# A two-layer metaformer on one core: the second convolution's weights are made between layer 0's expert tiles, and expert results load by half strips

## The chip, the cores and the metric

The kernel runs on one core of a Trainium2 chip. The metric is device time of one execution in microseconds (us). The time before is the median of three runs, 1847.21 us (1844.24 to 1854.55).

## The reference, cut to what matters

The input is x, (2, 256, 56, 56) in float32. Two layers follow each other; both add to x.

```python
# layer 0
x = x + attention(ln_c(x))                # 7x7 window attention, 8 heads
t = to_tokens(x)                          # (2, 3136, 256)
t = t + moe0(ln_t(t))                     # 8 experts, top 2: out = tokens + sum_e weight_e * expert_e(tokens)
x = from_tokens(t)
# layer 1
x = x + conv_block(ln_c(x))               # below
t = to_tokens(x)
t = t + moe1(ln_t(t))                     # 8 experts of width 512, top 2
x = from_tokens(t)

def noised_tri_conv(x, w):                # w: (256, 256, 3, 3)
    tq = ternary_quantize(w - mean(w))    # -1, 0 or 1, thresholds from the extremes of all of w
    return conv3x3(x, tq) + einsum('bchw,oc->bohw', x, tq[:, :, 1, 1])   # centre tap counts twice

def conv_block(x):
    out1 = relu(batch_norm(noised_tri_conv(x, w1)))
    out2 = batch_norm(noised_tri_conv(out1, w2))
    return relu(out1 + out2)
```

## The kernel before

The picture is cut into 14 strips of 8 rows (448 positions, four blocks of 112 tokens). The kernel goes through these stages: attention by strips; layer 0's experts; the first convolution; the second convolution; layer 1's routing by strips; layer 1's experts; the output.

**Layer 0's experts.** Tokens are sorted to their experts through memory, and 56 tiles of 256 rows are worked off one after another (`experts_in_order`). For each tile TensorE transposes (pt, L1073), ScalarE copies to ut (L1077), TensorE makes ph (L1105), ScalarE applies gelu into h (L1112), TensorE makes py (L1122), VectorE adds the bias into y (L1130), and GpSimd scatters y's rows to ys (L1132). The order of SyncE, VectorE, TensorE and ScalarE is that of the program here (`manual_schedule`). py has two buffers and y five.

**The ternary weights between the tiles.** From the tile on at which routing is done, `beside` advances the generator `prepare` by four steps after each tile. It runs `ternary` for w1, then for w2: each loads the weights piece by piece into space that later holds strips, takes their extremes and sum (L1250, L1252, L1255), and turns them into -1, 0 and 1 (L1286 to L1290). The end of `ternary` depends on the target. For w1 (four components of F(2,3)) it makes the transformed weights in bf16 (L1302 to L1309). For w2 the target has three components, and two ScalarE copies per 128x2304 (L1297) move the plain taps to `sums[1]` in bf16.

**The first convolution** (`conv`, L1771) works on pairs of strips in the row-wise form F(2,3): 28 steps, four components for each of seven pairs. `component` makes v on GpSimd (L1765), hi on ScalarE (L1766, the part of v that the fast matmul format holds) and lo = v - hi on VectorE (L1767); 24 matmuls (L1792) follow, and VectorE or ScalarE adds their result up in x (L1811 to L1820). v, hi and lo have two buffers each. Its own weights are cast to wq by ScalarE before (L1776).

**Combining beside it.** The strips come into being beside the steps. `combine(i)` reads the middle state x_mid, loads the expert results of a strip, 896 KB, in one DMA (`gathered`, L1172; three buffers `got`), adds them with their weights (`add_up`: on VectorE, L1191; for strip 2 on ScalarE, L1183, and GpSimd, L1186), takes the statistics of each token, normalizes into xn (L726; two buffers), transposes on TensorE (L1200) and copies into the padded picture pad (L1748). Strips 0 to 2 come before the first step, strips 3 and 4 during the first two steps, and then two strips for each pair of strips that is convolved. SyncE's order is that of the program; that of the other engines is chosen at compile time, in general the earliest in the program among what is ready.

**The second convolution** (`conv43`, L1844) uses F(4,3) with six components, on groups of 2, 4, 4 and 4 strips: 24 steps. Its weights wq4 (36,864 bytes a partition) are made by `weights43` (L1823), called at step 26 of the first convolution, once the pool of `combine` is closed: a GpSimd add (L1831), two ScalarE multiplies (L1833, L1834) and five VectorE passes (L1835 to L1839) over 128x1536. Between the convolutions `affine` makes scale and shift from the statistics (L1970 to L1977), and `between` (L2028) writes the rectified strips to pad on ScalarE. In a step, VectorE (with GpSimd for some parts) makes p, q, r, s and from them v in PSUM (two buffers), ScalarE hi (L1902) and VectorE lo (L1903); both have three buffers and are prepared two steps ahead. Their pool, conv_c2, takes the place of the first convolution's.

**After it**, `residual` reads x_mid again into back (L2068) and adds the transposed result to it (L2087).

Pools of fast memory are placed at both ends of the space and opened and closed like stacks, so that a tile that lies on an earlier one waits for that one's last use. On the low side, from the bottom: x_all, pad, sums[1] (134,592 to 143,808), the small tiles of the raw pool (to 145,376), conv_w1 with wq (to 169,952), conv_c1 with two each of hi, lo and v, 3,712 bytes each (to 192,224). On the high side, from 229,344 down: conv_t with got and xn (to 196,096), and after it wq4 (to 192,480). During layer 0's tiles the high side reaches down to 174,496, where the buffers xg begin.

Of the kernel before, what the change touches and what calls it, by code (L numbers as in the profile page):

```python
# [10 lines left out]
F32 = mybir.dt.float32  # L11
F32R = mybir.dt.float32r
# [620 lines left out]
def metaformer(ctx: ExitStack, tc: tile.TileContext, a: dict, out: bass.AP, flag):  # L633
# [532 lines left out]

        add_up(i, gathered(i, ys, tp, bufs), wgt, xt)

    def gathered(i, ys, tp, bufs=2):
        rows = NTT * TOP * TT  # L1170
        y = tp.tile([TT, NTT, TOP, C], F32, tag="got", name="got", bufs=bufs)
        nc.sync.dma_start(  # L1172
            y, ys[i * rows : (i + 1) * rows, :].rearrange("(p t j) c -> p t j c", t=NTT, j=TOP)
        )
        return y

    def add_up(i, y, wgt, xt, away=False):

        if away:
            for j in range(TOP):  # L1180
                for t in range(NTT):
                    n = i * NTT + t
                    nc.scalar.activation(  # L1183
                        y[:, t, j, :], y[:, t, j, :], AF.Copy, scale=wgt[:, j, n : n + 1]
                    )
                nc.gpsimd.tensor_tensor(xt, xt, y[:, :, j, :], ALU.add)  # L1186
            return
        for t in range(NTT):
            n = i * NTT + t
            for j in range(TOP):  # L1190
                nc.vector.scalar_tensor_tensor(  # L1191
                    xt[:, t, :], y[:, t, j, :], wgt[:, j, n : n + 1], xt[:, t, :], ALU.mult, ALU.add
                )

    def channels(ps, tag, xt):
# [34 lines left out]
    def ternary(name, sums, ps_pool, tag, tp, at):  # L1230

        size = KC * TAPS * C
        wide = NTT * C
        raw = x_all.rearrange("p s c -> p (s c)")[:, at * wide : at * wide + size]
        parts = [(n, raw[:, n : n + PART]) for n in range(0, size, PART)]

        def load(i):
            n = min(wide, size - i * wide)
            nc.sync.dma_start(raw[:, i * wide : i * wide + n], a[name + "_flat"][:, i * wide : i * wide + n])

        st3 = tp.tile([P, 3, len(parts)], F32, tag="st3", name="st3")
        load(0)
        for i, (n, part) in enumerate(parts):
            if n % wide == 0 and n + wide < size:
                load(n // wide + 1)
            nc.vector.tensor_reduce(st3[:, 0, i : i + 1], part, AX.X, ALU.max)  # L1250
            yield
            nc.vector.tensor_reduce(st3[:, 1, i : i + 1], part, AX.X, ALU.min, negate=True)  # L1252
            yield
            low = tp.tile([P, PART], F32, tag="low", name="low", bufs=1)
            nc.scalar.activation(low, part, AF.Copy, accum_out=st3[:, 2, i : i + 1])  # L1255
        st = tp.tile([P, 3], F32, tag="st", name="st")
        nc.vector.tensor_reduce(st[:, 0:2], st3[:, 0:2, :], AX.X, ALU.max)
# [12 lines left out]
        nc.vector.scalar_tensor_tensor(  # L1270
            lo, ext[:, 1:2], -1.0, mean, ALU.mult, ALU.subtract
        )
        span = tp.tile([P, 1], F32, tag="w_span", name="w_span")
        rest = tp.tile([P, 1], F32, tag="w_rest", name="w_rest")
        nc.vector.tensor_tensor(span, hi, lo, ALU.subtract)
        nc.vector.tensor_scalar_mul(third, span, 1.0 / 3.0)


        nc.vector.scalar_tensor_tensor(rest, third, -2.0, span, ALU.mult, ALU.add)
        nc.vector.tensor_tensor(rest, rest, third, ALU.subtract)  # L1280
        nc.vector.scalar_tensor_tensor(third, rest, 1.0 / 3.0, third, ALU.mult, ALU.add)
        nc.vector.tensor_tensor(lo, lo, third, ALU.add)
        nc.vector.tensor_tensor(hi, hi, third, ALU.subtract)
        for n, part in parts:
            low = tp.tile([P, PART], F32, tag="low", name="low", bufs=1)
            nc.vector.tensor_scalar(low, part, mean, lo, ALU.subtract, ALU.is_lt)  # L1286
            yield
            nc.vector.tensor_scalar(part, part, mean, hi, ALU.subtract, ALU.is_gt)
            yield
            nc.vector.tensor_tensor(part, part, low, ALU.subtract)  # L1290
            yield
        g = raw.rearrange("p (k y c) -> p k y c", k=KC, y=3)
        middle = g[:, :, 1, C : 2 * C]
        nc.vector.tensor_scalar_mul(middle, middle, 2.0)
        if sums.shape[2] == 3:
            for k in range(KC):
                nc.scalar.copy(sums[:, k], g[:, k])  # L1297
                yield
            return
        for k in range(KC):  # L1300
            up, middle, down = (g[:, k, y, :] for y in range(3))
            nc.scalar.copy(sums[:, k, 0, :], up)  # L1302
            nc.scalar.copy(sums[:, k, 3, :], down)
            nc.vector.tensor_tensor(up, up, down, ALU.add)
            yield
            nc.vector.tensor_scalar_mul(middle, middle, 0.5)
            yield
            for c, op in ((1, ALU.add), (2, ALU.subtract)):
                nc.vector.scalar_tensor_tensor(sums[:, k, c, :], up, 0.5, middle, ALU.mult, op)  # L1309
                yield  # L1310
# [4 lines left out]
    with ExitStack() as st:  # L1315
# [330 lines left out]
        def routed_all():  # L1646
# [32 lines left out]

            some = x_all[:, len(STRIPS) - 3 :].rearrange("p s c -> p (s c)").bitcast(BF16)  # L1680
            sums.append(some.rearrange("p (k n c) -> p k n c", k=KC, n=COMPS))
            sums.append(wqp.tile([P, KC, 3, 3 * C], BF16, tag="sums", name="sums"))

        def prepare():
            for i in range(2):
# [24 lines left out]
    with mid:  # L1710

        with ExitStack() as st:
# [20 lines left out]
            def combine(i):  # L1733

                xt = XT[STRIPS[i]][:TT]
                if i >= X_FIRST:
                    nc.sync.dma_start(xt, x_mid[i])
                got = gathered(i, ys[0], tp, 3)
                yield
                add_up(i, got, wgt0, xt, i == X_FIRST - 1)  # L1740
                yield
                rstd, nmr = yield from token_stats(tp, xt, eps6, True)
                xn = tp.tile([TT, NTT, C], F32, tag="xn", name="xn")
                scaled(xn, xt, rstd, nmr)
                yield
                pu = channels(strips_ps, "pu", xn)
# [73 lines left out]
                                nc.vector.bn_stats(stats[:, o, i, :], X[STRIPS[i]][:, o, :])  # L1820
                return stats

            def weights43(taps):  # L1823

                wp2 = st.enter_context(
                    tc.tile_pool(name="conv_w2", bufs=1, side="right", reuse_waits="tile")
                )
                w = wp2.tile([P, KC, COMPS4, 3 * C], F32R, tag="wq4", name="wq4")
                g = [taps[:, :, y, :] for y in range(3)]

                nc.gpsimd.tensor_tensor(w[:, :, 4, :], g[0], g[2], ALU.add)  # L1831
                both = w[:, :, 4, :].bitcast(F32)
                nc.scalar.mul(w[:, :, 0, :], g[0], 1.5)  # L1833
                nc.scalar.mul(w[:, :, 5, :], g[2], 6.0)  # L1834
                nc.vector.tensor_tensor(w[:, :, 1, :], both, g[1], ALU.add)  # L1835
                nc.vector.tensor_tensor(w[:, :, 2, :], both, g[1], ALU.subtract)
                nc.vector.scalar_tensor_tensor(g[0], g[0], 0.25, g[2], ALU.mult, ALU.add)
                for c, by in ((3, 0.5), (4, -0.5)):
                    nc.vector.scalar_tensor_tensor(  # L1839
                        w[:, :, c, :], g[1], by, g[0], ALU.mult, ALU.add  # L1840
                    )
                return w

            def conv43(wq, cp, vps, tp, at_step):  # L1844
# [6 lines left out]
                def component(u, c):  # L1851
# [20 lines left out]
                    def banks(ap):  # L1872
                        return ap[:, :n].rearrange("p (a r) k w -> p a (r k w)", r=4)

                    hi, lo = tile_of("hi", F32R, 3), tile_of("lo", F32R, 3)
                    pv = vps.tile([P, 2, 512], F32, tag="v", name="pv")
                    v = pv[:, : n // 4, : 4 * KC * WC]
                    if c == 1:
# [108 lines left out]
            def combining(n):  # L1987
# [18 lines left out]
                if late < 2 and 5 <= i < len(STRIPS):  # L2006
                    coming.append(combine(i))
                push_all()
                if n == COMPS * UNITS - 2:
                    assert not coming  # L2010
                    strips_on.close()
                    wq4.append(weights43(sums[1]))

            wq4 = []

            with tc.manual_schedule(engines={mybir.EngineType.SP}):
                stats = conv(sums[0], combining)
            scale, shift = affine(stats, bn["g1"], bn["b1"], rp)
            first_on.close()
            cp = st.enter_context(tc.tile_pool(name="conv_c2", bufs=2, reuse_waits="tile"))  # L2020
            vps = st.enter_context(tc.tile_pool(name="conv_vs", bufs=2, space=PSUM, reuse_waits="tile"))

# [17 lines left out]
                    for i in FOURS[u + 1]:  # L2040
                        between(i + 1)

            stats = conv43(wq4[0], cp, vps, rp, rectifying)
            scale2, shift2 = affine(stats, bn["g2"], bn["b2"], rt, eps5_36)
        wq_held.close()

# [244 lines left out]
```

## Time and profile before

| | |
|---|---|
| median of three runs | 1847.21 us |
| profiled execution | 1852.05 us, its span 1850.1 us |
| mean granted TensorE clock | 0.874 of full speed |
| TensorE busy (matmuls) | 1530.3 us, 83% of the span |
| VectorE busy | 979.4 us, 53% |
| ScalarE busy | 696.1 us, 38% |
| GpSimd busy | 655.1 us, 35% |
| DMA | 291.77 MB, mean 158 GB/s |

The stages, read from the timeline: attention to about 515 us, layer 0's tiles to 841, first convolution to 1040, second convolution to 1182, layer 1's routing to 1390, layer 1's experts to 1770, output to 1850.

A row of a timeline gives the start in us, the duration, the engine (PE is TensorE, DVE VectorE, ACT ScalarE, POOL GpSimd, SP SyncE), the line, the operation, its output and inputs by name and shape, and in brackets the idle time before it and what ended that. In the chain of waits each row is a piece of the one path that ended last. In a table of stretches the columns are the stretch, its length, then the busy time and the instruction count of PE, PEld, DVE, ACT and POOL, then the granted clock, the share of the DMA engines and GB/s.

### The profile page before, as it was taken

What the parts mean: (1) busy time and instruction counts of PE and PEld (TensorE: products, weight loads), DVE (VectorE), ACT (ScalarE), POOL (GpSimd) and SP (SyncE); (2) the same over time, 40 slices, a digit from 0 to 9 for tenths busy, and PEclk for the clock granted to TensorE, in tenths of its full rate; (3) what the DMA queues carried; (4) which work ended last, traced back from release to release, by engine and by line L of the source; (5) the groups of instructions that cost most, each with busy time, mean ns of one, the idle gap of its engine ahead of it and who ended that gap; (6) DMA issues with size and microseconds to landing.
All of it is one profiled execution on the core that took longest, in us unless ns stands there. A gap on an engine that the chain in (4) does not pass through costs nothing.

```text
span 1850.1 us, 25838 instructions
## 1 busy us (share of the span) xinstructions
PE 1530.3 (83%) x8612; PEld 1199.4 (65%) x8612; DVE 979.4 (53%) x2688; ACT 696.1 (38%) x1358; POOL 655.1 (35%) x664
## 2 busy tenths in 40 slices
PE   6999998999778669894899799666348999999963
PEld 3555555555467557783788688555337888888842
DVE  4467566465645337845999788666432111111136
ACT  3454442434333324643444532344213333333312
POOL 3112534335333654442344143164562222222210
PEclk9999988999889879995999899755558999999975
DMA  7022333213267667885551000133544778788758
GB/s 244 22 83 82 113 90 112 62 52 93 60 205 229 230 208 263 307 256 156 158 163 53 1 1 1 40 112 98 170 136 152 270 265 270 262 279 277 274 161 301
DMA packets 91886, 291.77 MB, mean 158 GB/s; under 512 B 20487, under 2 KB 35803, under 8 KB 80416
## 3 DMA queue, kind: packets, MB, share of 16 engines
q1 hardware_dynamic: 66736, 231.79, 40.5%
q0 software_dynamic: 21200, 51.82, 8.0%
q10 hardware_dynamic: 3808, 6.42, 1.0%
q8 instruction: 70, 1.15, 0.3%
q14 instruction: 72, 0.59, 0.1%
HBM read 218.51 MB, written 74.20 MB: 158 GB/s over the span
## 4 chain that ended last, share of the span: by engine, by line
PE 52%; DVE 21%; DMA 8%; issue 7%; another core or an unknown queue 5%; POOL 4%; ACT 3%; SPq 0%; POOLq 0%; ACTq 0%; DVEq 0%
PE ph L1105 14%; PE py L1122 12%; PE av L1486 5%; PE sc L1457 3%; PE pj L1409 3%; DVE x L1191 3%; PE pw L1556 3%; PE pv L1431 3%; PE pl L784 2%; PE pt L1073 2%; DMA got<-ys 2%; DMA out<-o_out 2%; DVE oc L1543 2%; DVE t_stats L705 2%
## 5 line engine op out<-in xcount | busy, mean ns | idle before, releaser
L1105 PE MATMUL ph<-ut,w 128*128 128x256 f32 (+1 forms) x1472 | 320.3, 370 | 28.2 <-issue 20.3
L1130 DVE TENSOR_TENSOR y<-py,w 128x512 f32<-128x512 f32 (+1 forms) x120 | 76.8, 640 | 439.2 <-PE py L1122 379.2
L1122 PE MATMUL py<-w,h 128*128 128x256 f32 x1288 | 298.8, 380 | 0.0
L1105 PEld LDWEIGHTS ph<-ut,w 128*128 128x128 f32 x1472 | 258.2, 200 | 59.8 <-issue 22.4
L870 POOL DMA_INDIRECT xs<-u,pos x224 | 217.1, 969 | 168.0 <-issue 87.0
L1122 PEld LDWEIGHTS py<-w,h 128*128 128x128 f32 x1288 | 244.8, 192 | 33.1
L1132 POOL DMA_INDIRECT ys<-y,dest x136 | 136.3, 1003 | 274.8 <-DVE dest L1080 185.5
L1112 ACT ACTIVATE h<-ph,w 128x256 f32<-128x256 f32 (+1 forms) x368 | 162.3, 447 | 131.2 <-PE ph L1105 82.2
L1476 ACT ACTIVATE ex<-sc 112x476 f32<-112x476 f32 (+3 forms) x224 | 116.7, 570 | 207.8 <-PE sc L1466 174.9
L1077 ACT COPY ut<-pt 128x512 f32<-128x512 f32 (+1 forms) x120 | 65.2, 543 | 302.5 <-PE pt L1073 244.9
L1486 PE MATMUL av<-ex,vals 112*64 112x238 f32 (+3 forms) x896 | 124.1, 397 | 17.8 <-DVE acc L1496 14.3
L1792 PE MATMUL pc<-lo,wq 128*128 128x448 f32 x336 | 132.2, 395 | 6.5 <-DVE lo L1767 6.4
L1496 DVE TENSOR_TENSOR acc<-av,acc 128x238 f32<-128x238 f32 (+3 forms) x224 | 87.8, 407 | 87.5 <-PE av L1486 65.3
L1792 PE MATMUL pc<-hi,wq 128*128 128x448 f32 x336 | 131.7, 394 | 2.0 <-DVE x L1816 1.8
L1132 POOL DMA_INDIRECT ys<-y,to x81 | 82.3, 1016 | 135.0 <-DVE dest L1080 76.4
L1191 DVE SCALAR_TENSOR_TENSOR x<-got,wgt,x 112x256 f32<-112x256 f32 x216 | 102.3, 544 | 30.4 <-DMA got<-ys 30.4
L1935 PE MATMUL pc<-hi,wq 128*128 128x448 f32 (+1 forms) x288 | 104.4, 371 | 15.9 <-ACT hi L1902 9.4
L1935 PE MATMUL pc<-lo,wq 128*128 128x448 f32 (+1 forms) x288 | 103.6, 368 | 0.2 <-DVE lo L1903 0.2
L1457 PE MATMUL sc<-q_im,keys 32*112 32x238 f32 (+3 forms) x896 | 94.3, 427 | 9.5 <-ACT ex L1476 5.7
L1486 PEld LDWEIGHTS av<-ex,vals 112*64 112x64 f32 x896 | 55.9, 141 | 67.7 <-issue 25.2
L1765 POOL TENSOR_TENSOR v<-pad 128x928 f32<-128x928 f32 (+1 forms) x28 | 56.4, 2028 | 99.4 <-DVE lo L1767 49.1
L1073 PE MATMUL pt<-ident,xg 128*128 128x128 f32 x434 | 71.7, 287 | 15.5 <-ACT ut L1077 10.4
(273 smaller groups left out, 2479.7 us busy)
## 6 DMA issues: line engine op xcount, KB each, us to landing
w<-in_L_experts SPq DMA_DIRECT2D x64, 1154.0 KB
w<-in_L_experts SPq DMA_DIRECT2D x56, 641.0 KB
xg<-xs SPq DMA_DIRECT2D x97, 260.0 KB
got<-ys SPq DMA_DIRECT2D x28, 896.0 KB
acc<-in_fresh SPq DMA_DIRECT2D x14, 896.0 KB
xt<-in_x_tok SPq DMA_DIRECT2D x14, 448.0 KB
xr<-in_x_tok SPq DMA_DIRECT2D x14, 448.0 KB
rec<-shares SPq DMA_DIRECT2D x28, 224.0 KB
```

Source lines behind the costliest of these rows:

```text
L870: w = nc.gpsimd.indirect_dma_start(xs[:, :], bass.IndirectOffsetOnAxis(ap=pos[:, j, t0 + t : t0 + t + 1], axis=0), us[t // NTT][:, t % NTT ...
L1073: nc.tensor.transpose(pt[:, k, i * P : (i + 1) * P], d["xg"][:, i, k * P : (k + 1) * P], ident)
L1105: nc.tensor.matmul(ph[:, :g], w1[:, k, f * P : (f + 1) * P], d["ut"][:, k, :g], start=k == 0, stop=k == KC - 1,)
L1112: nc.scalar.activation(d["h"][:, f, :g], ph[:, :g], AF.Gelu, bias=b1[:, f : f + 1])
L1122: nc.tensor.matmul(py[:, i, :], d["h"][:, f, i * P : (i + 1) * P], w2[:, f, :], start=f == 0, stop=f == NF - 1,)
L1132: o = nc.gpsimd.indirect_dma_start(ys[:, :], bass.IndirectOffsetOnAxis(ap=d["to"][:, i : i + 1], axis=0), y[:, i, :], None, bounds_check=T ...
L1191: nc.vector.scalar_tensor_tensor(xt[:, t, :], y[:, t, j, :], wgt[:, j, n : n + 1], xt[:, t, :], ALU.mult, ALU.add)
L1457: nc.tensor.matmul(sc[h // 2][:, h % 2, :nq], keys[g][p, c, tx * TT : (tx + 1) * TT], q_im[p, c, r0:r1, c0:c1], start=True, stop=False,)
L1476: nc.scalar.activation(e[:, :, :nq], sc[j][:, :, :nq], AF.Exp, scale=HD**-0.5)
L1486: nc.tensor.matmul(av[VW * i : VW * (i + 1), :nq], vals[g % 3][:, tx, 2 * c + j, 2 * i : 2 * i + 2, :].rearrange("p a d -> p (a d)"), ex[j ...
L1792: nc.tensor.matmul(pc[:, :NT], wq[:, k, c, dx * C + o * P : dx * C + (o + 1) * P], part[:, :, k, dx : dx + W], start=m == 0, stop=m == 2 * ...
L1935: nc.tensor.matmul(pc[:, : 2 * ns * W], wq[:, k, c, dx * C + o * P : dx * C + (o + 1) * P], part[:, : 2 * ns, k, dx : dx + W], start=m == ...
```

## The change

`ternary` now makes all six components of the F(4,3) weights for w2 between layer 0's tiles: per half of the channels two ScalarE multiplies and six VectorE passes over 128x768, in six steps of the generator instead of one. They wait in `sums[1]`, which grows from three to six components in bf16 (9,216 to 18,432 bytes a partition). `weights43` becomes six ScalarE casts from there to wq4; it is called after the first convolution, its `affine` and the closing of its pools. `combine` loads the results of a strip by two DMAs of two token blocks each, into five half buffers, with one buffer for xn; the adds of strip 2 on GpSimd go block by block. hi and lo of the second convolution have two buffers instead of three.

```diff
-    def gathered(i, ys, tp, bufs=2):
+    def gathered(i, ys, tp, bufs=2, step=NTT):
         rows = NTT * TOP * TT
...
+        src = ys[i * rows : (i + 1) * rows, :].rearrange("(p t j) c -> p t j c", t=NTT, j=TOP)
+        ts = []
+        for at in range(0, NTT, step):
+            y = tp.tile([TT, step, TOP, C], F32, tag="got", name="got", bufs=bufs)
+            nc.sync.dma_start(y, src[:, at : at + step])
+            ts += [y[:, t] for t in range(step)]
+        return ts
...
                     nc.scalar.activation(
-                        y[:, t, j, :], y[:, t, j, :], AF.Copy, scale=wgt[:, j, n : n + 1]
-                    )
-                nc.gpsimd.tensor_tensor(xt, xt, y[:, :, j, :], ALU.add)
+                        y[t][:, j, :], y[t][:, j, :], AF.Copy, scale=wgt[:, j, n : n + 1]
+                    )
+                    nc.gpsimd.tensor_tensor(xt[:, t, :], xt[:, t, :], y[t][:, j, :], ALU.add)
...
-        if sums.shape[2] == 3:
+        if sums.shape[2] == COMPS4:
             for k in range(KC):
-                nc.scalar.copy(sums[:, k], g[:, k])
+                up, middle, down = (g[:, k, y, :] for y in range(3))
+                part = [sums[:, k, c, :] for c in range(COMPS4)]
+                nc.scalar.mul(part[0], up, 1.5)
+                nc.scalar.mul(part[5], down, 6.0)
+                nc.vector.tensor_tensor(part[3], up, down, ALU.add)
                 yield
+                nc.vector.tensor_tensor(part[1], part[3], middle, ALU.add)
+                yield
+                nc.vector.tensor_tensor(part[2], part[3], middle, ALU.subtract)
+                yield
+                nc.vector.scalar_tensor_tensor(up, up, 0.25, down, ALU.mult, ALU.add)
+                yield
+                for c, by in ((3, 0.5), (4, -0.5)):
+                    nc.vector.scalar_tensor_tensor(part[c], middle, by, up, ALU.mult, ALU.add)
+                    yield
...
-            sums.append(wqp.tile([P, KC, 3, 3 * C], BF16, tag="sums", name="sums"))
+            sums.append(wqp.tile([P, KC, COMPS4, 3 * C], BF16, tag="sums", name="sums"))
...
-                got = gathered(i, ys[0], tp, 3)
+                got = gathered(i, ys[0], tp, 5, NTT // 2)
...
-                xn = tp.tile([TT, NTT, C], F32, tag="xn", name="xn")
+                xn = tp.tile([TT, NTT, C], F32, tag="xn", name="xn", bufs=1)
...
-            def weights43(taps):
+            def weights43(sums):
...
-                nc.gpsimd.tensor_tensor(w[:, :, 4, :], g[0], g[2], ALU.add)
-                both = w[:, :, 4, :].bitcast(F32)
-                nc.scalar.mul(w[:, :, 0, :], g[0], 1.5)
-                nc.scalar.mul(w[:, :, 5, :], g[2], 6.0)
-                nc.vector.tensor_tensor(w[:, :, 1, :], both, g[1], ALU.add)
-                nc.vector.tensor_tensor(w[:, :, 2, :], both, g[1], ALU.subtract)
-                nc.vector.scalar_tensor_tensor(g[0], g[0], 0.25, g[2], ALU.mult, ALU.add)
-                for c, by in ((3, 0.5), (4, -0.5)):
-                    nc.vector.scalar_tensor_tensor(
-                        w[:, :, c, :], g[1], by, g[0], ALU.mult, ALU.add
-                    )
+                for c in (1, 2, 3, 4, 0, 5):
+                    nc.scalar.copy(w[:, :, c, :], sums[:, :, c, :])
                 return w
...
-                    hi, lo = tile_of("hi", F32R, 3), tile_of("lo", F32R, 3)
+                    hi, lo = tile_of("hi", F32R), tile_of("lo", F32R)
...
-                if n == COMPS * UNITS - 2:
-                    assert not coming
-                    strips_on.close()
-                    wq4.append(weights43(sums[1]))
...
             scale, shift = affine(stats, bn["g1"], bn["b1"], rp)
             first_on.close()
+            strips_on.close()
+            wq4 = weights43(sums[1])
```

More of the change, by code (lines that the diff above doesn't have):

```diff
@@ L1167, in gather @@
         add_up(i, gathered(i, ys, tp, bufs), wgt, xt)
-    def gathered(i, ys, tp, bufs=2):
+    def gathered(i, ys, tp, bufs=2, step=NTT):
         rows = NTT * TOP * TT
-        y = tp.tile([TT, NTT, TOP, C], F32, tag="got", name="got", bufs=bufs)
-        nc.sync.dma_start(
-            y, ys[i * rows : (i + 1) * rows, :].rearrange("(p t j) c -> p t j c", t=NTT, j=TOP)
-        )
-        return y
+        src = ys[i * rows : (i + 1) * rows, :].rearrange("(p t j) c -> p t j c", t=NTT, j=TOP)
[5 more added lines that the diff above has]
+        return ts
     def add_up(i, y, wgt, xt, away=False):
@@ L1191, in add_up @@
                 nc.vector.scalar_tensor_tensor(
-                    xt[:, t, :], y[:, t, j, :], wgt[:, j, n : n + 1], xt[:, t, :], ALU.mult, ALU.add
+                    xt[:, t, :], y[t][:, j, :], wgt[:, j, n : n + 1], xt[:, t, :], ALU.mult, ALU.add
                 )
@@ L1828, in weights43 @@
                 w = wp2.tile([P, KC, COMPS4, 3 * C], F32R, tag="wq4", name="wq4")
-                g = [taps[:, :, y, :] for y in range(3)]
-                nc.gpsimd.tensor_tensor(w[:, :, 4, :], g[0], g[2], ALU.add)
-                both = w[:, :, 4, :].bitcast(F32)
-                nc.scalar.mul(w[:, :, 0, :], g[0], 1.5)
-                nc.scalar.mul(w[:, :, 5, :], g[2], 6.0)
-                nc.vector.tensor_tensor(w[:, :, 1, :], both, g[1], ALU.add)
-                nc.vector.tensor_tensor(w[:, :, 2, :], both, g[1], ALU.subtract)
-                nc.vector.scalar_tensor_tensor(g[0], g[0], 0.25, g[2], ALU.mult, ALU.add)
-                for c, by in ((3, 0.5), (4, -0.5)):
-                    nc.vector.scalar_tensor_tensor(
-                        w[:, :, c, :], g[1], by, g[0], ALU.mult, ALU.add
-                    )
+                for c in (1, 2, 3, 4, 0, 5):
+                    nc.scalar.copy(w[:, :, c, :], sums[:, :, c, :])
                 return w
@@ L2008, in combining @@
                 push_all()
-                if n == COMPS * UNITS - 2:
-                    assert not coming
-                    strips_on.close()
-                    wq4.append(weights43(sums[1]))
-            wq4 = []
             with tc.manual_schedule(engines={mybir.EngineType.SP}):
@@ L2041, in rectifying @@
                         between(i + 1)
-            stats = conv43(wq4[0], cp, vps, rp, rectifying)
+            stats = conv43(wq4, cp, vps, rp, rectifying)
             scale2, shift2 = affine(stats, bn["g2"], bn["b2"], rt, eps5_36)
```

## The prediction

> **What bounds the kernel now.** I read the busy slices first: TensorE is on for 83% of the span, so what counts is where it stops. Then the chain of waits, and then the engine timelines around every stop that the change touches. There are five.
>
> (1) Layer 0's tiles. TensorE's timeline (start, duration, idle before in brackets):
>
> ```profile
> 803.27 1.89 PE L1122 MATMUL py<-w,h 128*128 128x256 f32 x8
> 808.24 1.11 PE L1073 MATMUL pt<-ident,xg 128*128 128x128 f32 x4 [3.08 <-ACT ut L1077]
> 809.15 3.62 PE L1105 MATMUL ph<-ut,w 128*128 128x256 f32 x8
> 812.56 2.71 PE L1122 MATMUL py<-w,h 128*128 128x256 f32 x8
> 815.11 0.60 PE L1073 MATMUL pt<-ident,xg 128*128 128x128 f32 x4
> ```
>
> and ScalarE's beside it:
>
> ```profile
> 803.58 4.12 ACT L1297 CAST sums<-x 128x2304 bf16<-128x2304 f32 x2 [3.53 <-DVE x L1294]
> ```
>
> A tile normally takes 3.89 us (py 799.38 to 803.27). Here two casts stand in ScalarE's queue ahead of ut, TensorE waits, and afterwards it runs slowly (ph 3.62 instead of 1.89). Transposes due at 805.00 and 808.89 came so late that the second began at 815.11: 6.2 us lost.
>
> (2) The start of the first convolution, from the chain of waits:
>
> ```profile
> 841.38 5.89 DMA got<-ys
> ...
> 861.20 2.36 POOL x L1186
> ...
> 865.89 12.67 DMA got<-ys
> ...
> 882.80 9.88 DMA got<-ys
> ```
>
> Three times the end of a load of results sets the time, and once GpSimd's last add for strip 2. After it VectorE is full:
>
> ```profile
> 900.00:1003.00 103.00, 100.30 (x491) 86.43 (x492) 101.51 (x238) 49.09 (x88) 41.73 (x22) 0.98 0.48 135
> ```
>
> The third busy figure is VectorE: 101.51 of 103 us. What the start gains is thus kept to 1003.
>
> (3) From 1003 to 1040 TensorE sets the pace, with small holes where VectorE, busy with the second convolution's weights, made lo late:
>
> ```profile
> 1011.92 0.48 PE L1792 MATMUL pc<-lo,wq 128*128 128x448 f32 x1 [0.69 <-DVE lo L1767]
> 1023.73 0.47 PE L1792 MATMUL pc<-lo,wq 128*128 128x448 f32 x1 [0.93 <-DVE lo L1767]
> 1029.70 0.48 PE L1792 MATMUL pc<-lo,wq 128*128 128x448 f32 x1 [0.55 <-DVE lo L1767]
> ```
>
> (4) Between the convolutions ScalarE leads: it is idle, then the square root, then the rectified strips, and TensorE waits for its hi.
>
> ```profile
> 1042.53 0.29 ACT L1973 ACTIVATE scale<-mv,eps 128x2 f32<-128x2 f32 x1 [12.73 <-DVE mv L1970]
> 1043.64 5.32 ACT L2028 ACTIVATE pad<-x,shift,scale 128x448 f32<-128x448 f32 x8 [0.82 <-DVE shift L1977]
> ```
>
> ```profile
> 1049.45 0.77 PE L1935 MATMUL pc<-hi,wq 128*128 128x224 f32 x2 [9.37 <-ACT hi L1902]
> ```
>
> (5) In the second convolution the waits show that ScalarE's hi is made as early as three buffers allow:
>
> ```profile
> ACT hi L1902 <- PE pc L1935: 29.0, 10, 4.8
> ```
>
> **Part by part.** All durations are of the profiled execution: 1852.05 us, span 1850.1 and 1.95 around it. It lies 4.84 above the median of the three runs, 1847.21; I take differences from it and subtract them from the median.
>
> *Weights made between tiles.* Removed: the two 2.06 us casts and the 6.2 us stall. Added: twelve VectorE passes over 128x768 (rows of w1's own end: 0.95 us, the next starting 0.87 later) and four ScalarE multiplies (L1302's cast of that shape: 0.82). Four steps go with each tile, so VectorE has 4 x 0.87 + 0.61 for y + 0.67 for dest, to and held = 4.8 us in a tile of 3.89 and falls 0.9 behind in each of three tiles, 2.7 in all. What waits for y is py two tiles later: 2 x 3.89 - 1.73 - 0.6 = 5.4 us of cover, so that costs nothing; without cover it would cost 2.7. Two multiplies fit into ScalarE's 1.74 us idle ahead of ut. They wait for no late pass, as the casts did for L1294. I leave 0.5 for a slip: -5.7, between -6.2 and -3.5.
>
> The first convolution's four casts to wq (L1776, 1.47 each) ran at 747 to 756, among the tiles. With the sums 9,216 bytes a partition larger, wq moves up by as much in the layout of before (to 154,592 to 179,168) and onto the first xg buffers (from 174,496), so they wait for the last tiles. ScalarE is idle for 19.24 us before 852: 0, between -0.5 and +1.5.
>
> *Half strips.* While the first strips load, DMA moves 276 to 293 GB/s; half a strip, 458,752 bytes, takes 1.6 us of that, so the first adds start 1.6 earlier. Strip 2 goes over ScalarE and GpSimd: two GpSimd adds of 2.34 become eight over 112x256. No such row exists; GpSimd's 928 elements took 2.19 and 464 took 1.19, that is 2.16 ns an element and 0.19 beside it, so an estimate of 0.74 each, 5.9 together instead of 4.7. But the first starts after one multiply, not four: about 852.8 instead of 855.60, and the last two after the delayed multiplies, ending at about 859.2 instead of 863.55: -4.3. The SyncE queue holds x_mid's store of strip 2 ahead of the loads of strips 3 and 4, so those issue 4.3 earlier as well, and at 892.77 VectorE (idle 2.74) can begin on the first half, 1.6 earlier. Together -5.9, between -8 and 0. Five halves are enough: the sixth waits for the first strip's first half, free at about 847. That halts only SyncE's queue, whose next item, x_mid's store of strip 0, isn't due yet. The fourteen added issues on that queue (L1172's median is 0.46) fall into its idle time: 0. One xn buffer: the second strip's normalization may start when the first one's transposes end (891.9) and its own were not begun before 894.84: 0.
>
> [...] The row: 896 KB landed 5.89 us after issue, with others in flight. [...]
>
> *The first convolution's tail.* POOL's and VectorE's weight passes go, so the holes of 0.69 + 0.93 + 0.55 close: -2.2, between -2.7 and 0.
>
> *Casts by ScalarE.* Six of 128x1536, bf16 to f32r (L1776: 1.47, next start 1.38 later). Source ready; target not: conv_c1 now ends at 201,440 and wq4 begins at 192,480, so wq4 lies on both v buffers and the end of the second lo, which the last of 28 steps reads. The casts therefore start when the last matmul ends (1040.1 in this trace) and, being written ahead of the rectified strips, go ahead of them: 6 x 1.38 + 0.3 for the root = 8.6, strips at +8.7 instead of +3.5 after that matmul. Behind them are queued eight strips' activations, then hi, then TensorE: +5.2, between 0 (they run before, or fall behind) and +8.3 (all exposed).
>
> *hi and lo from three buffers to two.* The ten waits of (5) now last one step longer. After a step's last matmul come hi 0.94 and lo 1.11, within the next step's 5.1 us, if VectorE is free. The nearest row is the tail of (3): two buffers, VectorE 31.1 busy of 37, 2.2 us lost in 7 steps; for 24 steps 7.5. Here the passes ahead of hi still run two steps early in PSUM, so I take less than half: +3.0, between 0 and +9.
>
> *back.* x_mid's read at 1181.98 waited for small tiles of the raw pool; moved up, back lies on the old sums only and loads early. Next late are the transposes (1182.58 + 2.34): x at 1185.0, not 1186.16: -1.1, between -1.1 and 0.
>
> Sum: -5.7 - 5.9 - 2.2 + 5.2 + 3.0 - 1.1 = **-6.7**: 1845.4 profiled, **1840.5** as median. Its own range, 1834 to 1847.
>
> **The rivals.** *A: the casts hide.* If ScalarE's order puts the strips first or wq4 is free earlier, the +5.2 goes: -11.9, 1835.3. For it: 12.73 us idle before the root. Against it: the overlap with the last lo. *B: halves bring nothing* and cost nothing, since the whole set of strips must pass the same DMA engines: -0.8, 1846.4. For it: 276 to 293 GB/s is steady already. Against it: VectorE waits for the first strip alone, and GpSimd's add is in the chain. *C, slower: two buffers starve TensorE.* If VectorE takes a step's four x passes (0.61 each) and one p or q pass (3.15) before lo, lo ends 0.9 + 2.4 + 3.15 + 1.1 = 7.6 us after the last matmul, 2.5 more than a step; in half of 18 wide steps that is 22 us: -9.7 + 22 = +12.3, 1859.5. It decides from the point where lo starts over 4 us after the step's end. Against it: ScalarE's hi runs ahead now, and VectorE has 20 us idle in 102. *D: the casts between tiles stall TensorE after all*, as w1's end did (2.21 at 757.16): inside the first term's range.
>
> **How the numbers follow.** Main case 0.48, A 0.22, B 0.19, C 0.11. A measurement of this kernel tells 0.5%, 9.2 us, from no change. Faster by more: of the main case about 0.35 (terms near their favourable ends), of A 0.85, of B 0.05: 0.37. Slower by more: C, nearly all, and 0.01 of the rest: 0.11. Within: 0.52. The range 1829 to 1853 takes in A with good terms and B with bad ones and leaves out C and a little below.
>
> **What would show it.** Right: no stop near 803 and three tiles of about 3.9 us with VectorE full; x L1186 eight times, ended 4 us earlier after got; no hole in lo before the first convolution's end; six casts of 1.4 us straight after its last matmul and the strips some 5 us later than now; hi waiting for pc in most steps, TensorE's holes there under 4 us; back issued long before it is needed. Wrong: the casts before 1040, or py waiting for y, or lo waited for in each step.

## The result, and the profile after

The changed kernel takes 1856.3 us (median of 20 runs, 1848.33 to 1866.52); the kernel before, run beside it, 1854.19 us (20 runs). The ratio is 1.0015 with a 95% interval of 0.9995 to 1.0034: a difference of +2.8 us, between -0.9 and +6.3, that can't be told from no change. The prediction said 1840.5. Of the 15.8 us between, 7.0 lie in the base (the three runs it started from had the median 1847.21, the twenty 1854.19); the rest is in the terms, -6.7 where it should have been about +2.

The profiled execution after took 1856.27 us (span 1854.5). Single executions differ by several us ahead of the change (w2's first psum_w matmul begins at 771.89 us in the profile before, at 775.28 after), so stages are compared by their own lengths, between events of TensorE's timeline (from start to start, where nothing else is said):

| stretch | before | after | predicted |
|---|---|---|---|
| w2's first psum_w matmul to the end of the last py of layer 0 | 64.13 | 59.24 | -5.7 |
| first issue of got to the first matmul of convolution 1 | 27.98 | 23.56 | -4.3 |
| convolution 1, first to last matmul | 170.35 | 170.21 | -1.6 - 2.2 |
| its last matmul to the first of convolution 2 | 9.74 | 14.63 | +5.2 |
| convolution 2, first to last matmul | 124.42 | 130.11 | +3.0 |
| its last matmul to the second strip's pt of layer 1 | 18.76 | 19.10 | -1.1 |

**Layer 0's tiles** have no stop any more behind w2's psum_w. ScalarE's timeline shows the new multiplies between gelu and ut, and TensorE's the tiles behind them at 3.89 us each:

```profile
804.67 0.84 ACT L1301 ACTIVATE sums<-x 128x768 bf16<-128x768 f32 x1
805.41 0.83 ACT L1302 ACTIVATE sums<-x 128x768 bf16<-128x768 f32 x1
806.52 0.59 ACT L1077 COPY ut<-pt 128x512 f32<-128x512 f32 x1 [0.28 <-PE pt L1073]
```

```profile
805.83 0.60 PE L1073 MATMUL pt<-ident,xg 128*128 128x128 f32 x4
...
809.72 0.60 PE L1073 MATMUL pt<-ident,xg 128*128 128x128 f32 x4
...
813.61 0.60 PE L1073 MATMUL pt<-ident,xg 128*128 128x128 f32 x4
```

**The start of convolution 1.** GpSimd's eight adds end at 857.61, 17.7 us after the first issue of got (839.88), where the two of before ended 22.2 us after it:

```profile
851.14 6.47 POOL L1188 TENSOR_TENSOR x<-x,got 112x256 f32<-112x256 f32 x8 [12.53 <-ACT got L1185]
```

**Convolution 1.** The holes of 0.69, 0.93 and 0.55 at its end are gone, but TensorE now waits in front of transposes, which it didn't do there before:

```profile
926.81 0.41 PE L1202 MATMUL pu<-ident,xn 112*128 112x112 f32 x2 [0.56 <-ACT xn L726]
...
994.55 1.89 PE L1202 MATMUL pu<-ident,xn 112*128 112x112 f32 x8 [1.67 <-ACT xn L726]
```

There are six such waits: 0.56 + 0.56 + 0.27 + 0.49 + 0.55 + 1.67 = 4.1 us.

**Between the convolutions** ScalarE's timeline has the casts just as the prediction placed them, from the end of the last matmul (1033.65 + 0.37) on, and the strips behind them, 8.5 us after that matmul instead of 3.5:

```profile
1034.05 2.84 ACT L1845 CAST wq<-sums 128x1536 fp32r<-128x1536 bf16 x2 [9.50 <-PE pc L1807]
1036.80 0.29 ACT L1977 ACTIVATE scale<-mv,eps 128x2 f32<-128x2 f32 x1
1037.00 5.57 ACT L1845 CAST wq<-sums 128x1536 fp32r<-128x1536 bf16 x4
1042.48 5.32 ACT L2028 ACTIVATE pad<-x,shift,scale 128x448 f32<-128x448 f32 x8
```

**Convolution 2.** In the waits, hi stands behind pc thirteen times instead of ten, 47.8 us instead of 29.0; TensorE's timeline shows what it costs:

```profile
1058.53 0.37 PE L1939 MATMUL pc<-hi,wq 128*128 128x224 f32 x1 [1.37 <-ACT hi L1906]
...
1079.53 0.47 PE L1939 MATMUL pc<-hi,wq 128*128 128x448 f32 x1 [2.74 <-ACT hi L1906]
```

ScalarE's timeline says why. hi isn't late by its own 0.9 us. With two buffers its place comes free one step later, and by then it stands in ScalarE's queue behind whatever was put there meanwhile: six rectified strips, or a multiplication that waits for GpSimd:

```profile
1054.02 4.04 ACT L2028 ACTIVATE pad<-x,shift,scale 128x448 f32<-128x448 f32 x6
1057.95 0.53 ACT L1906 CAST hi<-pv 128x464 fp32r<-128x464 f32 x1
...
1078.08 0.58 ACT L1966 ACTIVATE x<-x 128x448 f32<-128x448 f32 x1 [4.35 <-POOL x L1964]
1078.56 0.91 ACT L1906 CAST hi<-pv 128x928 fp32r<-128x928 f32 x1
```

In the kernel before, hi of the same step ran ahead of these multiplications:

```profile
1070.15 0.94 ACT L1902 CAST hi<-pv 128x928 fp32r<-128x928 f32 x1 [4.16 <-PE pc L1935]
1073.54 0.58 ACT L1958 ACTIVATE x<-x 128x448 f32<-128x448 f32 x1 [2.45 <-DVE x L1949]
```

After the change TensorE waits for hi at four steps (1.37, 1.07, 2.74 and 1.72 us). At all four the v that hi reads had been written, and the last matmul on hi's buffer had ended, 3.7 to 5.9 us before hi began (at 1074.11 for the one that began at 1078.56). So what these four wait for in the end is the queue; the missing third buffer is why they stand so far back in it.

**After it**, back is issued at 1167.52, long before it is needed, as predicted. But GpSimd's last sum of convolution 2 now ends later, and VectorE's last sum, with the statistics behind it, waits for it:

```profile
1179.80 0.62 DVE L1957 TENSOR_TENSOR x<-x,pc 128x448 f32<-128x448 f32 x1 [4.07 <-POOL x L1967]
```

### The profile page after: what moved, and what is told of

Read it like the earlier page. It is cut to its first block, busy times and chain, and to the rows that moved or that the text cites. A ratio compares the mean times of both kernels' runs of the same rounds, so it can differ in the third digit from the quotient of the medians.

```text
span 1854.5 us, 25881 instructions
## 1 busy us (share of the span) xinstructions
PE 1534.2 (83%) x8612; PEld 1200.2 (65%) x8612; DVE 976.3 (53%) x2695; ACT 701.2 (38%) x1364; POOL 654.4 (35%) x669
## 5 line engine op out<-in xcount | busy, mean ns | idle before, releaser
L1122 PE MATMUL py<-w,h 128*128 128x256 f32 x1288 | 303.4, 385 | 0.0
L1132 POOL DMA_INDIRECT ys<-y,dest x136 | 136.4, 1003 | 278.1 <-DVE dest L1080 186.6
L1807 PE MATMUL pc<-lo,wq 128*128 128x448 f32 x336 | 130.2, 388 | 4.6 <-DVE lo L1782 4.5
L1807 PE MATMUL pc<-hi,wq 128*128 128x448 f32 x336 | 130.4, 389 | 1.1 <-ACT hi L1781 1.1
L1193 DVE SCALAR_TENSOR_TENSOR x<-got,wgt,x 112x256 f32<-112x256 f32 x216 | 96.1, 512 | 27.2 <-DMA got<-ys 27.1
```

The source lines that it names most:

```text
L1122: nc.tensor.matmul(py[:, i, :], d["h"][:, f, i * P : (i + 1) * P], w2[:, f, :], start=f == 0, stop=f == NF - 1,)
L1132: o = nc.gpsimd.indirect_dma_start(ys[:, :], bass.IndirectOffsetOnAxis(ap=d["to"][:, i : i + 1], axis=0), y[:, i, :], None, bounds_check=T ...
L1193: nc.vector.scalar_tensor_tensor(xt[:, t, :], y[t][:, j, :], wgt[:, j, n : n + 1], xt[:, t, :], ALU.mult, ALU.add)
L1807: nc.tensor.matmul(pc[:, :NT], wq[:, k, c, dx * C + o * P : dx * C + (o + 1) * P], part[:, :, k, dx : dx + W], start=m == 0, stop=m == 2 * ...
```

## The experiments

The theory that this result suggests (theory 1): the gains of 4 to 5 us at two places were real, and two buffers (+6) and casts on the path (+5) ate them. What was unclear is why convolution 1 didn't get shorter. All experiments in one table, the same stretches as above (tiles; start; convolution 1; gap; convolution 2; to layer 1), and the ratio to the kernel before:

| kernel | tiles | start | conv 1 | gap | conv 2 | to layer 1 | ratio (95%) |
|---|---|---|---|---|---|---|---|
| b_halves | 61.21 | 24.31 | 171.66 | 9.73 | 124.42 | 19.08 | 0.9980 (0.9959 to 1.0001) |
| b_xn1 | 61.21 | 27.91 | 170.03 | 9.73 | 124.45 | 19.11 | 0.9977 (0.9953 to 1.0001) |
| b_two | 61.21 | 27.94 | 170.15 | 9.73 | 130.69 | 20.40 | 1.0056 (1.0022 to 1.0090) |
| a_xn2 | 58.53 | 24.44 | 169.33 | 14.63 | 130.03 | 19.10 | 1.0005 (0.9982 to 1.0027) |
| a_three | 57.91 | 23.25 | 170.42 | 14.63 | 124.40 | 17.65 | 0.9983 (0.9964 to 1.0002) |
| a_tail | 56.88 | 23.44 | 169.46 | 10.07 | 130.69 | 19.11 | 0.9985 (0.9961 to 1.0009) |
| a_nmr | 56.94 | 23.13 | 167.03 | 14.63 | 128.67 | 19.11 | 1.0004 (0.9987 to 1.0020) |
| b_nmr | 61.21 | 26.32 | 171.88 | 9.73 | 124.45 | 18.96 | 0.9989 (0.9967 to 1.0010) |
| a_mul | 57.91 | 24.15 | 169.19 | 14.65 | 138.73 | 24.71 | 1.0127 (1.0014 to 1.0239) |
| a_best | 56.88 | 24.23 | 168.80 | 10.07 | 124.42 | 17.65 | 0.9962 (0.9942 to 0.9981) |
| a_best2 | 58.45 | 24.14 | 166.65 | 10.06 | 124.42 | 17.64 | 0.9937 (0.9913 to 0.9961) |

The gap and the second convolution repeat closely where nothing in them was changed (9.73 in four kernels, 14.63 to 14.65 in five, 124.40 to 124.45 in seven); the whole time doesn't. Convolution 1 repeats less well: 168.80 to 170.42 in the changed kernel and the five made from it whose nmr is the old one. So causes are read from the stretches, and the ratio only confirms.

**Two buffers for hi and lo.** First in the kernel before, alone:

```diff
-                    hi, lo = tile_of("hi", F32R, 3), tile_of("lo", F32R, 3)
+                    hi, lo = tile_of("hi", F32R), tile_of("lo", F32R)
```

> The kernel before with two hi and two lo buffers in the second convolution instead of three and nothing else. Theory 1: the buffers alone are the late hi of the profile after the change; the second convolution, 124.42 us from its first to its last matmul, grows by 5 to 6 us to about 130, lost before its eighth step and at one step near 1145. Rival (the late hi came from ScalarE's order after the weight casts, not from the buffers): at most 126.

130.69: the buffers alone make the loss, +6.3, and the last sums of GpSimd another 1.3 to 1.6 behind it (20.40 instead of 18.76, or of 18.96 to 19.11 in the other kernels with the old code there). Then the third buffer put back into the changed kernel:

```diff
-            rp = st.enter_context(tc.tile_pool(name="raw", bufs=1, reuse_waits="tile"))
+            rp = st.enter_context(tc.tile_pool(name="raw", bufs=1, side="right", reuse_waits="tile"))
...
-                    hi, lo = tile_of("hi", F32R), tile_of("lo", F32R)
+                    hi, lo = tile_of("hi", F32R, 3), tile_of("lo", F32R, 3)
...
             wq4 = weights43(sums[1])
+            wq_held.close()
             cp = st.enter_context(tc.tile_pool(name="conv_c2", bufs=2, reuse_waits="tile"))
```

> The changed kernel with three hi and three lo buffers again (the small tiles of the raw pool lie at the other end, and the space of the bf16 weights is given back after the casts). Theory 1 (the buffers alone are what the second convolution lost): its 130.11 us fall to about 124.4, the whole is about 6 us faster than the change. Rival (bf16 weights or the later casts disturb it too): 127 or more.

124.40, and 17.65 behind it: both losses go. The 17.65 is 1.1 to 1.5 less than with the late read of back (18.76 to 19.11); the prediction gave the early read 1.1.

**The multiplications ahead of hi.** To see whether ScalarE's queue makes hi late, the three multiplications L1962, L1963 and L1966 went to GpSimd:

```diff
-                        nc.scalar.mul(both(3), both(3), 2.0)
+                        nc.gpsimd.tensor_scalar_mul(both(3), both(3), 2.0)
```

> The changed kernel (two hi and lo buffers) with the three multiplications at the end of a group of the second convolution (L1962, L1963, L1966) on GpSimd instead of ScalarE, so that no instruction that waits for GpSimd stands ahead of hi in ScalarE's queue. Theory 3: with two buffers hi becomes ready late, and what is queued ahead of it decides; the waits of TensorE at 1079.53 (2.74 and 0.68) and 1145.14 (1.72 and 0.68) come from that queue, and the second convolution falls from 130.11 us to about 126; the early waits (1.37, 0.30, 1.07, 0.30), behind rectified strips, stay. Rival (hi is late because its buffer comes free late): 129 to 130.

The expectation of the whole failed: 138.73. GpSimd took 1.3 to 3.3 us for each multiplication, its r, s and sums came late, and TensorE waited for VectorE's x instead (2.51 and 5.97). The waits for hi at the two places did go, and those of 1.42 and 1.10 behind the rectified strips stayed, which fits the queue; but so much else moved that this run alone is support and not proof. Its ratio rests on two executions.

**The casts.** wq4 becomes six tiles; four lie above the first convolution's pool and are cast when the last strip is combined, two after the last matmul:

```diff
+                if n == COMPS * UNITS - 2:
+                    assert not coming
+                    strips_on.close()
+                    weights43(sums[1], (1, 2, 3, 4))
...
             first_on.close()
-            strips_on.close()
-            wq4 = weights43(sums[1])
+            weights43(sums[1], (0, 5))
```

> The changed kernel with wq4 as six tiles: the four components used first lie above conv_c1 and are cast beside the first convolution's last steps, where ScalarE is idle for 9.5 us; the other two after its last matmul. Theory 1 (the wait for the shared space is what puts the casts on the path): the gap from the last matmul of the first convolution to the first of the second falls from 14.63 to about 10 (9.74 before), and the convolution ahead stays within 1 us of 170.2; the whole is 4 to 5 us faster than the change. Rival (ScalarE's casts only move their delay to hi of the last steps): the gap falls but the first convolution grows by 2 us or more.

The gap is 10.07. ScalarE's timeline of this kernel has the casts where it used to be idle, and the remaining two beside `affine`:

```profile
995.33 4.21 ACT L1845 CAST wq<-sums 128x1536 fp32r<-128x1536 bf16 x3
999.91 0.97 ACT L1781 CAST hi<-v 128x928 fp32r<-128x928 f32 x1 [0.37 <-PE pc L1807]
1000.79 1.47 ACT L1845 CAST wq<-sums 128x1536 fp32r<-128x1536 bf16 x1
...
1031.03 2.85 ACT L1845 CAST wq<-sums 128x1536 fp32r<-128x1536 bf16 x2 [9.50 <-PE pc L1807]
```

The convolution ahead didn't grow (169.46). So it was the wait for the last matmul, and not the amount of casting, that put 4.6 us on the path. This kernel has the call earlier in the program as well as the tiles elsewhere; that the space is what made the casts wait is read from the changed kernel, where the first cast is released by that matmul (9.50 <-PE pc L1807).

**Convolution 1: half strips and xn.** Three kernels: the half strips alone, one xn buffer alone, and the changed kernel with two xn buffers and four halves:

```diff
-                got = gathered(i, ys[0], tp, 3)
+                got = gathered(i, ys[0], tp, 5, NTT // 2)
```

> The kernel before with the half strips alone (five half buffers, xn still two). Measured from the first issue of got to the first matmul of the first convolution (before 27.98 us, after the change 23.56), and from there to its last matmul (170.35 and 170.21). Theory 1 (one xn buffer ate what the halves brought): the first stretch falls to about 23.6 and the second stays at 170 to 171, so that the convolution ends about 4 us earlier. Rival (VectorE is full in the convolution and gives the early start back whatever the buffers): 23.6 and about 174.5, no gain at its end.

```diff
-                xn = tp.tile([TT, NTT, C], F32, tag="xn", name="xn")
+                xn = tp.tile([TT, NTT, C], F32, tag="xn", name="xn", bufs=1)
```

> The kernel before with one xn buffer instead of two and nothing else. Theory 1: TensorE waits for xn in front of transposes in the middle of the first convolution, as in the profile after the change (0.56 + 0.56 + 0.27 + 0.55 + 1.67 = 3.6 us), and the 170.35 us from its first to its last matmul become about 174. Rival: 170 to 171, as the prediction said (one buffer costs nothing).

```diff
-                got = gathered(i, ys[0], tp, 5, NTT // 2)
+                got = gathered(i, ys[0], tp, 4, NTT // 2)
...
-                xn = tp.tile([TT, NTT, C], F32, tag="xn", name="xn", bufs=1)
+                xn = tp.tile([TT, NTT, C], F32, tag="xn", name="xn")
```

> The changed kernel with two xn buffers and four instead of five half buffers of got. Theory 1: the waits for xn in the first convolution go, 170.21 us become about 166.6, and the whole is 3.6 us faster than the change. Rival (VectorE full): 170 again. If four half buffers are too few, the stretch before the first matmul (23.56) grows instead.

Theory 1 falls for xn: one buffer costs nothing (170.03), and two bring start and convolution together nothing (24.44 + 169.33 = 193.77 us, as after the change). The half strips alone win 3.7 us at the start and give 1.3 back in the convolution (171.66, between what theory 1 and its rival expected), with TensorE's waits for xn in it though xn has its two buffers there (0.55, 0.53, 0.22, 0.55, 0.56, 1.60). So the waits came with the half strips. The largest can be followed through the engines of b_halves; VectorE, GpSimd, TensorE:

```profile
989.90 1.80 DVE L716 TENSOR_TENSOR t_nmr<-t_nmr,t_rstd 112x4 f32<-112x4 f32 x1
```

```profile
989.53 2.16 POOL L1767 TENSOR_TENSOR v<-pad 128x928 f32<-128x928 f32 x1 [2.67 <-DVE lo L1769]
```

```profile
992.40 1.89 PE L1202 MATMUL pu<-ident,xn 112*128 112x112 f32 x8 [1.60 <-ACT xn L726]
```

t_nmr has four elements a partition and takes 0.15 us where no GpSimd pass runs beside it. Here it ends when GpSimd's v ends (991.70 and 991.69); ScalarE's xn waits for it, and TensorE for xn. In the same kernel three lo took 2.35 to 2.36 instead of 1.11 beside v (a fourth beside GpSimd's weight pass took 3.82). In the profile before no lo took over 1.13 us. There it was adds that took long beside v, those of strip 5 more than twice as long as those of strip 4; VectorE, then GpSimd:

```profile
878.65 3.25 DVE L1191 SCALAR_TENSOR_TENSOR x<-got,wgt,x 112x256 f32<-112x256 f32 x8 [0.86 <-DMA got<-ys]
...
892.77 7.10 DVE L1191 SCALAR_TENSOR_TENSOR x<-got,wgt,x 112x256 f32<-112x256 f32 x8 [2.74 <-DMA got<-ys]
```

```profile
893.10 4.52 POOL L1765 TENSOR_TENSOR v<-pad 128x928 f32<-128x928 f32 x2 [29.55 <-ACT pad L1748]
```

Taken as what the adds, lo and t_nmr of convolution 1 took beyond their time alone, VectorE stood still for about as long before the change (14.7 us, an estimate, all of it in adds) as after (15.0: 7.6 in adds, 4.7 in lo, 2.7 in t_nmr). What differs is which passes it hits.

**The stand-still.** So theory 2, put together from these rows (t_nmr 1.80 us for 0.15, lo 2.35 for 1.11, the eight adds of a strip 7.10 for 3.25): VectorE passes that read two inputs from fast memory stand still while GpSimd's v, or another of its passes, runs. One such pass was written in another form, in the changed kernel and in the kernel before:

```diff
-            nc.vector.tensor_tensor(nmr, nmr, rstd, ALU.mult)
+            for t in range(NTT):
+                nc.vector.tensor_scalar_mul(nmr[:, t : t + 1], nmr[:, t : t + 1], rstd[:, t : t + 1])
```

> The changed kernel with one VectorE pass of combine in another form: nmr = nmr * rstd (112x4, two inputs from fast memory, L716) becomes four passes of a column times a scalar. Theory 2: the early start is partly given back in the first convolution because VectorE passes with two inputs from fast memory stand still while GpSimd's v runs (t_nmr 0.16 alone, 1.80 beside it, and TensorE then waits 1.67 for xn). Then the wait of TensorE ahead of the last transposes (1.67) goes and the 170.21 us fall to 168 to 169. Rival (the order of the engines decides, not the stand-still): the hole stays or moves and the stretch stays within 0.7 of 170.2.

> The kernel before with nmr by four one-column passes and nothing else. Two of its fourteen t_nmr passes stood beside GpSimd's v, one for 2.21 us, but no wait of TensorE followed from them. Theory 2: the first convolution, 170.35 us, changes by less than 1 us. Rival (the passes cost in every order): 167 to 168.

Convolution 1 falls to 167.03 in the changed kernel; of the waits for xn one of 0.26 is left. All 56 new passes took 0.19 to 0.21 us, the 12 that ran beside GpSimd too. Theory 2 expected 168 to 169.

In the kernel before the expectation failed in its details: convolution 1 grew by 1.5 us (171.88), and the start fell by 1.7 (26.32). The 2.21 us pass of before had stood beside GpSimd's first add for strip 2 and lay on the chain to its second one, which now follows 1.45 us after the first one's end instead of 3.25. But what the start gained was given back: start and convolution together are 198.20 us, against 198.33.

How far the changed kernel is ahead of the kernel before, counted from the first issue of got, shows the place: 5.1 us where the 21st step of convolution 1 begins, and 1.3 where the 23rd does. The largest wait for xn lies between. All seven profiles with half strips and the old nmr lose 2.3 to 3.9 us there; the two with the new nmr (a_nmr and a_best2) lose 0.2. What stays open is how much of the 3.2 us is the stand-still itself: the order of the engines is made anew at each compilation, and it changed too. The gain isn't seen in a_nmr's ratio, which is within its uncertainty.

**Both mends, and with nmr.**

> Both mends in one kernel: three hi and lo buffers and the casts in the first convolution's tail. If the two losses add up, as theory 1 has it, it is 5.7 + 4.6 = about 10 us faster than the change and 6 to 9 us faster than the kernel before (0.3 to 0.5%). Rival (what is gained is lost again further on, in layer 1): less than 3 us faster than the kernel before.

> The kernel with both mends and, besides, nmr by four one-column passes. If the stand-still of t_nmr beside GpSimd's v is a loss of its own (3.2 us in the first convolution of the changed kernel), the 168.80 us of the first convolution fall to 166 to 167 here too, and the whole is 8 to 11 us faster than the kernel before (ratio about 0.995). Rival (those 3.2 us came with one particular order of the engines): 168.8 again and the ratio of the kernel with both mends, 0.996.

The losses add up: the gap is 10.07 and convolution 2 is 124.42 in one kernel, and the ratio is 0.9962 (0.9942 to 0.9981). With nmr, convolution 1 is 166.65, and the ratio 0.9937 (0.9913 to 0.9961): 11.7 us faster than the kernel before (7 to 16), a little more than the 8 to 11 expected. This version beats both kernels. From the first issue of got to the second strip's pt it takes 342.91 us, before 351.25, after the change 357.61.

## Why the prediction was right and wrong

- **Weights made between tiles: right in kind, -5.7 too large.** Behind w2's psum_w nothing stalls TensorE any more and VectorE's lag is covered, as worked out. But the 6.2 us belonged to one execution: a stop of 3.08 us and then 3 us lost at half rate (granted clock 0.50 from 807.4 to 814.2, and ph 3.62 us instead of 1.89). Four more profiles with the old code have the same stop, and full rate after it. From b_xn1:

```profile
809.67 0.66 PE L1073 MATMUL pt<-ident,xg 128*128 128x128 f32 x4 [3.08 <-ACT ut L1077]
810.16 1.89 PE L1105 MATMUL ph<-ut,w 128*128 128x256 f32 x8
```

  The tiles' stretch is 61.21 us in all four. With the new code it is 57.91 in a_three and a_mul, which ran just as slowly behind w2's psum_w: -3.3 for the stop alone. Averaged over the five profiles with the old code and the eight with the new one the difference is -4.0, but that takes in whether TensorE fell to half rate behind psum_w, which it did in nine of the thirteen.
- **wq's casts moved behind the tiles: right, 0.** They ran from 831.48 to 837.06, before the first results landed.
- **Half strips at the start: right.** -4.3 was predicted to the first matmul, -4.4 and (alone) -3.7 measured; the first add followed the first issue by 4.31 us instead of 5.99, 1.7 earlier where 1.6 was worked out. Two loads for a strip in place of one lost nothing that shows: after the change the first five were issued one behind the other from 839.88 to 841.64.
- **"What the start gains is thus kept to 1003": the step that failed first.** The 1.6 us at strip 5 and the 2.2 us at the tail were to shorten convolution 1 by 3.8, and it kept its length. The term of the half strips was -5.9; alone (b_halves) they brought 2.4 us to the end of convolution 1 (195.97 against 198.33). The tail's 2.2 came: the three holes closed, and the change is 2.2 us ahead of b_halves (193.77). But the order that the compiler made for the half strips put lo and t_nmr beside GpSimd's v, and by the 23rd step only 1.3 us of the gain was left. A table of stretches that showed VectorE busy for 101.51 of 103 us was read as work that only has to be done. Standing still counts as busy in it: nine of the 112x256 adds in that stretch ran beside GpSimd and took 1.68 us on average, the others 0.47, so about 11 of the 101.51 us (an estimate) are stand-still, in the profile before already.
- **Casts at the transition: right.** +5.2 predicted for the reason given (the space shared with the last lo), +4.9 measured; a_tail takes the reason away and 4.6 of it goes. Rival A is out for the kernel as changed.
- **hi and lo: the term that was most wrong.** +3.0 was taken from a range of 0 to +9; 5.6 to 6.3 was measured in the convolution in four kernels (4.2 in a_nmr), and about 1.5 more behind it. The working asked only whether VectorE is free when a step ends. It left out what stands ahead of hi on its own engine: up to six strips' activations and multiplications that wait for GpSimd. That is the mechanism of rival C, late hi and lo, on ScalarE instead of VectorE and at about a quarter of the 22 us that it was given.
- **back: right, and hidden.** -1.1 shows once three buffers are there (17.65); in the changed kernel the late sums of GpSimd cover it: 19.10, against 18.76 to 19.11 with the late read.

With these sizes the sum is -3.3 - 4.4 - 0.1 + 4.9 + 5.7 + 0.3 = +3.1, and the ratio gave +2.8. "Within 0.5%" was the likeliest of the three classes, and it came so, but on the other side of zero than the sum.

## What to carry to other kernels

The dropped buffers were paid here on the engine that fills the next one (ScalarE's hi; 5.6 to 6.3 us of convolution 2 in four kernels): look at what is queued ahead there, in order, and not only at whether some engine is free in the step. Where two gains and two losses of 4 to 6 us cancel, the losses are worth a second look: here both were consequences of where tiles lay in memory, and moving one small pool and splitting one tile turned a change of +2.8 us into -7 and, with one small pass rewritten, -11.7. The stall's price belonged to the execution it was read from (6.2 us there, 3.3 in four others); and three runs of a kernel whose runs spread over 20 us are a base that can be 7 us off.

## What was unexpected of the hardware

- **VectorE beside GpSimd.** lo (two inputs from fast memory) took 1.11 us alone and up to 2.36 beside v after the change; t_nmr 0.15 and up to 1.81, before the change 2.21; x<-x,pc, whose second input lies in PSUM, took 0.61 us alone and beside GpSimd (after the change, 27 passes with under a tenth and 25 with over half of their time beside a GpSimd pass). Not every pass was hit: the t_nmr at 938.60 before the change took 0.17 us inside a v, and the one at 929.05 in a_three 0.15. What took longer beside GpSimd in these rows had two inputs from fast memory. Passes with one mostly did not: t_stats of combine took 0.41 us alone and 0.40 beside it before the change (medians), the one-column passes 0.19 to 0.21 in all cases; a single t_nmr<-t_mv (L710) took 0.34 instead of 0.16 after it.
- **Half rate followed some stops and not others.** After the stop of 2.84 to 2.90 us at w2's psum_w, the next ph took 2.8 to 3.6 us instead of 1.89 in nine of the thirteen profiles, and 1.89 in four; after the stop of 3.08 us it did in one of five. The granted clock says the same: 0.50 from 773.3 to 776.7 in the profile before and from 774.6 to 781.5 after the change, 1.00 from 774 to 781 in a_tail. What decides it is not shown by any run.
